# The sum over scan directions: former directions added by TensorE in the collecting bank, the result copied out by ScalarE one unit later

## The chip, the cores and the metric

The kernel runs on one core of a Trainium2 chip. The metric is the device time of one launch in microseconds; the time before is the median of three runs. A core has TensorE (PE in the profile, its weight loads PEld), VectorE (DVE), ScalarE (ACT), GpSimd (POOL) and SyncE (SP), which here issues nearly all DMAs. Each engine works through its own instructions in order and waits on semaphores for the others.

## The reference, cut to what matters

Four layers are applied in turn to a batch of four images of 96 channels and 64 by 64 pixels: an attention, a selective scan block with gates and convolutions (layer 1), a sharpening convolution, and a second selective scan block (layer 3). What the change touches is the same in layers 1 and 3: a recurrence is run over the 4096 pixels in four orders, and the four results are added at each pixel.

```python
def step(h, inp):
    d, uu, bb, cc = inp
    h = h * jnp.exp(d[..., None] * A) + (d * uu)[..., None] * bb[:, :, None, :]
    y = jnp.einsum('bkdn,bkn->bkd', h, cc)
    return (h, y)
...
return jnp.moveaxis(ys, 0, -1) + u * D[None, :, :, None]
...
y = oy[:, 0] + inv[:, 0] + why + invwhy
```

Here `oy[:, 0]` is the order by rows, `why` by columns, and `inv` and `invwhy` the same two from the last pixel to the first. There are 192 channels (two halves of 96) and 16 states for each channel. Layer 1 has `+ Ds` in place of `u * D`, a constant for each channel.

## The kernel before, in words

`streams` holds one long schedule, written out by hand. There are eight scans, one for each image and layer (`SCANS`, line 37). A scan has 32 groups: four directions, four chunks of 1024 pixels, two halves of the channels (`groups`, line 1929). A group has 12 units, each for 8 channels with their 16 states on 128 partitions; so there are 3072 units. Layer 1 takes its directions in the order rows forward, rows back, columns forward, columns back; layer 3 takes columns forward, columns back, rows forward, rows back (`KINDS`, line 1927).

A unit `i` does this (`unit`, line 2160). A DMA brings the step sizes, spread over 128 partitions (`rep`, 512 KB, `fetch`, four units ahead). ScalarE takes their exponential (`decays`, two units ahead). TensorE spreads the input over 128 partitions into a PSUM tile (`drive`, two bf16 matmuls into `bx`, two units ahead). VectorE multiplies `bx` by B in place (`times_b`, line 2086, one unit ahead) and runs the recurrence (`scan`, line 2093). GpSimd multiplies by C (`times_c`, line 2105). ScalarE keeps the last column for the next chunk (`carry_on`, line 2101). After every fourth unit TensorE adds up the 16 states of four units into the PSUM tile `acc` (`collect`, lines 2107 to 2123). `acc` has one buffer. Of a group's three collects the first starts the sums and the last ends them; since they come five units late, those of group `g` fall into the units 5 and 9 of the group and 1 of the next.

When a group's sums are complete, `output` (line 2125) makes the image `yo` [128 x 1024] of them, and SyncE stores it at the start of the next unit (`store`, line 2141):

- In a back direction (128 of the 256 groups) the sum of the direction before has been read back from HBM into `yo` (line 2114, issued with the group's first collect), and VectorE adds `acc`, read in reverse (line 2132).
- In layer 3's rows forward (32 groups) `yo` has been loaded with the input `u` (line 2117), and VectorE forms `u * D + acc` (line 2138).
- In columns forward (64 groups) ScalarE copies `acc` (line 2134), and in layer 1's rows forward (32 groups) ScalarE copies it and adds the constant D (line 2136).

There is one `yo`. The output is the last thing that a unit issues on its engine but for the work below.

Beside the units runs other work: the layers before and after the scans of other images (`BESIDE`, line 38), as Python generators that are advanced in slots. A generator yields nothing after matmuls, a number after the steps that follow them, and a tuple inside a convolution. What may be begun in a unit is set by a budget: each unit adds `PACE[s]` us of TensorE's time to what is owed (line 2268, capped at 0.6 us carried over), and `mm` (line 1017) books the cost of each matmul in `spent`, 0.853 us for an f32 matmul of 512 columns. `prepare` makes the inputs of the group after next in the same slots. What is left of a scan's side work 19 units before the scan's end is issued at once (line 2266, `at == per - NG - LEAD - 1`, unit 365 of 384). `weave` (line 1307) interleaves several generators, as in `skip` (line 1694), of which four run at a time: a convolution and Silu, a matmul and Relu, a matmul and Tanh into its own PSUM tile (line 1710, followed by `yield 0.5`), and a VectorE step that reads that tile (line 1712). Side work and `prepare` share two PSUM tiles, `one`.

Of the kernel before, what the change touches and what calls it, by code (L numbers as in the profile page):

```python
# [9 lines left out]
F32 = mybir.dt.float32  # L10
BF16 = mybir.dt.bfloat16
AF = mybir.ActivationFunctionType
ALU = mybir.AluOpType
# [16 lines left out]
PCH = 512  # L30
# [870 lines left out]
def streams(ctx: ExitStack, tc: tile.TileContext, x, wts, cst, out, wat, cat, flag):  # L901
# [3 lines left out]
    nc = tc.nc  # L905
    keep = ctx.enter_context(tc.tile_pool(name="keep", bufs=1))
# [20 lines left out]
    def cv(name):  # L927
        n, m, shape = cat[name]
        return _view(ct, (n if n < n0 else n - n1 + n0, m, shape))
# [65 lines left out]
    ident, group = cv("ident"), cv("group")  # L995
# [14 lines left out]
    spent = [0.0]  # L1010

    def full(v):

        (step, _), *rest = v.ap
        return bass.AP(v.tensor, v.offset, [(step, 128), *rest])

    def mm(o, lhsT, rhs, first=True, last=True):

        lhsT, rhs = lhsT[:], rhs[:]
        if lhsT.shape[0] == 96 and lhsT.tensor.name in padded and rhs.tensor.name in padded:  # L1020
            lhsT, rhs = full(lhsT), full(rhs)
        n = 1
        for d in rhs.shape[1:]:
            n *= d
        m = o.shape[0]
        passes = 1 if rhs.dtype == BF16 else 1.07 if m == 32 else 2 if m == R + 2 * N else 4
        spent[0] += n * passes / 2400
        nc.tensor.matmul(o, lhsT=lhsT, rhs=rhs, start=first, stop=last)  # L1028
# [56 lines left out]
    decay, dsum = {}, {}  # L1085
    top_rate = derived(4, 2)
    with Stack(1) as T:
        t0 = T.tile([128, cst.shape[1] - n2], F32, name="t0")
        nc.scalar.dma_start(out=t0, in_=cst[:, n2:])
        n, m, shape = wat["l1_alog"]  # L1090
# [4 lines left out]
        n, m, shape = cat["spread"]  # L1095
        nc.vector.tensor_copy(spread.rearrange("p a b -> p (a b)"), t0[:, n - n2 : n - n2 + m])
        for tag in ("l1_", "l3_"):
            decay[tag] = keep.tile([128, 4, E // 8], F32, name=tag + "decay")
            n, m, shape = cat[tag + "alogn"]
# [207 lines left out]
    def weave(made, depth):  # L1307

        left, active = list(made), []
        while left or active:  # L1310
            if left and len(active) < depth:
                active.append(left.pop(0))
            for g in list(active):
                while True:
                    try:
                        v = next(g)
                    except StopIteration:
                        active.remove(g)
                        break
                    yield v  # L1320
                    if v is not None and not isinstance(v, tuple):
                        break

    def attention(b, xn, w, samp, dist):
# [442 lines left out]
    def finish(PX, b, V, blocks):  # L1767

        with Stack(2) as pool:
# [140 lines left out]
            for j in range(8):  # L1910
# [14 lines left out]
    NG = 96 // 8  # L1925
# [3 lines left out]
    groups = [(s, b, tag, k, axis, back, c, h) for s, (tag, b) in enumerate(SCANS)  # L1929
              for k, axis, back in KINDS[tag] for c in range(NCH) for h in range(2)]  # L1930
    carry = keep.tile([128, 2, NG], F32, name="carry")
    yo = keep.tile([128, CH], F32, name="yo")
    nc.gpsimd.memset(yo, 0.0)
    sums = keep.tile([96, len(SCANS), 4, 2, 2 * NCH], F32, name="sums")
# [3 lines left out]
    low, ready, live = {}, {}, {}  # L1938

    def time(t, back, j0, n):  # L1940

        if not back:
            return t[:, j0 : j0 + n]
        a = t.shape[1] - 1 - j0
        return t[:, a : (a - n if a >= n else None) : -1]

    def natural(c, back):
        return bass.ts(NCH - 1 - c if back else c, CH)
# [106 lines left out]
    def place(i):  # L2055


        g, m = divmod(i, NG)
        return g, m % 4 * 3 + m // 4

    def fetch(i):

        g, m = place(i)
        rep = sp.tile([128, CH], F32, name="rep", bufs=12)
        nc.sync.dma_start(out=rep, in_=ready[g][1][8 * m : 8 * m + 8, :].unsqueeze(0).to_broadcast([N, 8, CH]))
        live[i] = [rep]

    def decays(i):
        g, m = place(i)
        k, h = groups[g][3], groups[g][7]  # L2070
        tag = groups[g][2]
        a = live[i][0]
        nc.scalar.activation(a, a, AF.Exp, scale=decay[tag][:, k, NG * h + m : NG * h + m + 1])  # L2073

    def drive(i):

        g, m = place(i)
        parts = ready[g][0]
        bx = ps.tile([128, CH], F32, tag="bx", name="bx")
        for e in range(2):  # L2080
            mm(bx[:, bass.ts(e, PCH)], spread[:, m % 4, :], parts[:, m // 4, bass.ts(e, PCH)])
        live[i].append(bx)

    def times_b(i):
        bx = live[i][1]
        nc.vector.tensor_mul(bx, bx, ready[i // NG][2][:, 0, :])  # L2086

    def scan(i):
        g, m = divmod(i, NG)
        c, h = groups[g][6:]  # L2090
        a, bx = live[i]
        hs = sp.tile([128, CH], F32, name="hs", bufs=3)
        nc.vector.tensor_tensor_scan(out=hs, data0=a, data1=bx, initial=carry[:, h, m : m + 1] if c else 0.0,  # L2093
                                     op0=ALU.mult, op1=ALU.add)
        live[i] = a, hs

    def carry_on(i):
        g, m = divmod(i, NG)
        c, h = groups[g][6:]
        if c < NCH - 1:  # L2100
            nc.scalar.copy(carry[:, h, m : m + 1], live[i][1][:, CH - 1 : CH])  # L2101

    def times_c(i):
        a, hs = live[i]
        nc.gpsimd.tensor_tensor(a, hs, ready[i // NG][2][:, 1, :], ALU.mult)  # L2105

    def collect(i):

        g, m = divmod(i, NG)
        s, b, tag, k, axis, back, c, h = groups[g]  # L2110
        if m == 0:
            live["acc"] = ps.tile([128, CH], F32, tag="acc", name="acc", bufs=1)
            if back:
                nc.sync.dma_start(out=yo, in_=(y_row if axis == "r" else y_col)[h][b][:, natural(c, back)])
            elif axis == "r" and tag == "l3_":
                for q in range(4):
                    nc.sync.dma_start(out=yo[32 * q : 32 * q + 24],
                                      in_=u_row[h][b][24 * q : 24 * q + 24, natural(c, back)])
        hs = [live.pop(i + q)[0] for q in range(4)]
        w = addn[:, 24 - 8 * (m // 4) : 56 - 8 * (m // 4)]  # L2120
        for e in range(2):
            for q in range(4):
                mm(live["acc"][bass.ts(q, 32), bass.ts(e, PCH)], w, hs[q][:, bass.ts(e, PCH)], m == 0, m == NG - 4)

    def output(i):

        g, m = divmod(i, NG)
        s, b, tag, k, axis, back, c, h = groups[g]
        dst = (y_row if axis == "r" else y_col)[h][b][:, natural(c, back)]
        ya = time(live["acc"], back, 0, CH)  # L2130
        if back:
            nc.vector.tensor_add(yo, yo, ya)
        elif axis == "c":
            nc.scalar.copy(yo, ya)
        elif tag == "l1_":
            nc.scalar.activation(yo, ya, AF.Identity, bias=dsum[tag][:, h : h + 1])
        else:
            nc.vector.scalar_tensor_tensor(out=yo, in0=yo, scalar=dsum[tag][:, h : h + 1], in1=ya,
                                           op0=ALU.mult, op1=ALU.add)
        ready.pop(g)  # L2140
        return lambda: nc.sync.dma_start(out=dst, in_=yo)

# [1 line left out]
    DRIVE, SUM, SLOT = 0.43, 1.71, 0.5  # L2144
    total = len(groups) * NG
    per = total // len(SCANS)
    store, waiting, stored, owed = [], [], [0], 0.0

    def later(n, f):

# [2 lines left out]
    def catch_up(n):  # L2153
        for w in waiting:
            w[0] -= n
        for w in [w for w in waiting if w[0] <= 0]:
            waiting.remove(w)
            w[1]()

    def unit(i, prep, work, budget):  # L2160


        if i + AHEAD < total:
            fetch(i + AHEAD)
        while store:
            store.pop()()
            stored[0] += 1
        catch_up(1)
        j = i - BEHIND - 3
        due = j >= 0 and j % 4 == 0  # L2170
        left = budget - DRIVE - (SUM if due else 0.0)
        mine = 1 <= prep.slots <= 3
        left -= prep.begin(1.0) if mine else work.begin(left)
        if i + 2 < total:
            decays(i + 2)
        scan(i)
        if i:
            carry_on(i - 1)
        times_c(i)
        if i + 1 < total:  # L2180
            times_b(i + 1)
        if mine:
            prep.end()
        work.end()
        left -= work.begin(left)
        if due:
            collect(j)
        if i + 2 < total:
            drive(i + 2)
        work.end()  # L2190
        left -= work.begin(left)
        if due and j % NG == NG - 4:
            store.append(output(j))
        work.end()
        if not mine:
            prep.begin(1.0)
            prep.end()
        return left
# [41 lines left out]
    with tc.manual_schedule():  # L2240
# [15 lines left out]
        for i in range(total):  # L2256
            s, at = divmod(i, per)
            g, m = divmod(i, NG)
            if at == 0:
                work, owed = Slots(beside(s)), 0.0  # L2260
# [7 lines left out]
            owed = min(owed, 0.6) + PACE[s]  # L2268
            owed = unit(i, prep, work, owed)
# [16 lines left out]
    m = small.tile([128, 1], F32, name="worst_1")  # L2286
# [3 lines left out]
    w = small.tile([1, 2], F32, name="worst_2")  # L2290
# [35 lines left out]
```

## Time and profile before

| what | value |
|---|---|
| median of 3 runs | 13741.8 us (13741.55 to 13748.16) |
| the profiled execution | 13771.14 us, of which the span 13769.2 us |
| granted TensorE clock over the span | 0.901 |
| the eight scans | 647.7 to 13644.7 us of the span |
| GpSimd busy | 10280.4 us (75%) |
| DMA | 2682.51 MB, 195 GB/s |

The span runs from the first to the last instruction. Busy times of one engine are unions of its instructions; TensorE's ends are modelled, and its records overlap one another. In the lists of groups the columns are: line, engine, operation, output and inputs with their shapes, the count, then busy us and mean ns of one, then the idle time of the engine ahead of them and who ended it. All matmuls have line 1028, that of their helper; `acc<-rep,ct` are the collects, `bx<-parts,spread` the drives, `one<-...` and `held<-...` side work. An f32 matmul of the program stands as two records (768 collects of 8 matmuls are 12288 records), a bf16 one as one (3072 drives of 2 are 6144).

### The profile page before, as it was taken

How to read it: one execution, taken by the hardware profiler on the slowest of the kernel's cores; microseconds unless marked ns; L12 is line 12 of the kernel's file. 1: busy time of each engine (PE TensorE's matmuls, PEld its weight loads, DVE VectorE, ACT ScalarE, POOL GpSimd, SP SyncE). 2: the span in 40 equal slices, each digit the busy share in tenths (PEclk: the TensorE clock that was granted, in tenths of full speed). 3: DMA queues.
4: the chain of work that ended last, by engine and by line, in shares of the span. 5: the costliest groups of instructions: out<-in, count | busy, mean ns of one | idle time of the engine just before them, and what ended most of it. 6: DMA issues, size and time to landing. Idle time of an engine off the chain costs nothing. (4 is left out here: it accounts for less than half of the span.)

```text
span 13769.2 us, 128385 instructions
## 1 busy us (share of the span) xinstructions
PE 11150.4 (81%) x40802; PEld 3349.2 (24%) x40802; DVE 11633.7 (84%) x7509; ACT 8718.5 (63%) x12338; POOL 10280.4 (75%) x4730
## 2 busy tenths in 40 slices
PE   9888886988779896888868887898969887777756
PEld 3322221322223221222212221232313222111111
DVE  1488998998889988889988898898889988887886
ACT  3366576667756676665766566667756676665654
POOL 1178887888878877788877888787878878666674
PEclk9899998999889897999989998998979998888867
DMA  0277788787878888778877788797888878777674
GB/s 11 68 172 197 200 224 215 201 218 203 224 195 223 210 210 212 188 194 214 232 190 198 195 216 227 192 228 198 213 214 204 224 201 229 185 196 188 172 195 115
DMA packets 840849, 2682.51 MB, mean 195 GB/s; under 512 B 111264, under 2 KB 113792, under 8 KB 840160
## 3 DMA queue, kind: packets, MB, share of 16 engines
q1 hardware_dynamic: 839504, 2672.34, 76.2%
q8 instruction: 324, 5.31, 0.2%
q14 instruction: 365, 2.99, 0.1%
q10 hardware_dynamic: 656, 1.87, 0.0%
HBM read 2179.90 MB, written 493.88 MB: 194 GB/s over the span
## 5 line engine op out<-in xcount | busy, mean ns | idle before, releaser
L2105 POOL TENSOR_TENSOR rep<-hs,bc 128x1024 f32<-128x1024 f32 x3072 | 7221.1, 2357 | 2404.3 <-DVE hs L2093 2012.5
L1028 PE MATMUL one<-arena 128*96 128x512 f32 (+5 forms) x11072 | 5294.0, 604 | 583.9 <-ACT arena L1394 134.2
L2093 DVE TENSOR_TENSOR_SCAN hs<-rep,carry,bx 128x1024 f32<-128x1024 f32 x2304 | 5400.8, 2344 | 302.1 <-ACT rep L2073 36.2
L2086 DVE TENSOR_TENSOR bx<-bx,bc 128x1024 f32<-128x1024 f32 x3072 | 3717.8, 1210 | 683.6 <-PE bx L1028 677.9
L2073 ACT ACTIVATE rep<-rep,l_decay 128x1024 f32<-128x1024 f32 x3072 | 3496.2, 1143 | 764.1 <-DMA rep<-dd 743.3
L1028 PE MATMUL bx<-parts,spread 128*128 128x512 bf16 x6144 | 2030.3, 415 | 1338.7 <-DVE hs L2093 1225.9
L1028 PEld LDWEIGHTS one<-arena 128*96 128x96 f32 (+4 forms) x11072 | 1793.8, 172 | 3053.6 <-issue 1783.9
L2093 DVE TENSOR_TENSOR_SCAN hs<-rep,bx 128x1024 f32<-128x1024 f32 x768 | 1754.5, 2285 | 138.6 <-ACT carry L2101 57.8
L1028 PE MATMUL acc<-rep,ct 128*32 128x512 f32 x12288 | 1721.9, 674 | 7.0 <-POOL rep L2105 7.0
L1028 PEld LDWEIGHTS <-spread 128*128 128x128 bf16 x6144 | 446.9, 100 | 3663.4 <-DVE hs L2093 2374.3
L1028 PE MATMUL one<-pr,ct 64*96 64x512 f32 x1024 | 628.5, 698 | 76.1 <-ACT pr L1980 27.0
L1394 ACT ACTIVATE arena<-one 128x512 f32<-128x512 f32 x576 | 342.2, 594 | 495.3 <-PE one L1028 493.7
L1028 PEld LDWEIGHTS acc<-rep,ct 128*32 128x32 f32 x12288 | 359.4, 118 | 1169.3 <-issue 944.6
L2073 ACT ACT_TABLE_LOAD x492 | 631.2, 1283 | 8.8
L2101 ACT COPY carry<-hs 128x1 f32<-128x1 f32 x2304 | 408.7, 177 | 219.6 <-DVE hs L2093 216.9
L1028 PE MATMUL bx<-arena 128*96 128x512 f32 (+5 forms) x1120 | 489.2, 575 | 21.3 <-ACT arena L1808 3.2
L1028 PE MATMUL one<-arena,ct 128*96 128x512 f32 x508 | 293.9, 686 | 255.3 <-ACT arena L1546 194.5
L1028 PE MATMUL held<-arena,cols 128*32 128x256 f32 x3072 | 481.2, 395 | 12.3 <-ACT arena L1394 11.5
L1028 PE MATMUL held<-arena 128*32 128x256 f32 x3072 | 481.7, 395 | 0.0
L982 POOL MEMSET arena<- 32x1024 f32 (+5 forms) x81 | 54.0, 690 | 393.6 <-ACT arena L1394 321.5
L2015 ACT ACT_TABLE_LOAD x256 | 328.4, 1283 | 4.4
L1028 PE MATMUL one<-us,wt 128*38 128x512 f32 x1024 | 282.3, 674 | 49.1 <-DMA us<-urow 23.7
(3322 smaller groups left out, 9879.5 us busy)
## 6 DMA issues: line engine op xcount, KB each, us to landing
rep<-dd SPq DMA_DIRECT2D x3072, 512.0 KB
parts<-du SPq DMA_DIRECT2D x1024, 144.0 KB
bc<-rows SPq DMA_DIRECT2D x256, 512.0 KB
dd<-delta SPq DMA_DIRECT2D x256, 384.0 KB
du<-cut SPq DMA_DIRECT2D x256, 384.0 KB
yrow<-yo SPq DMA_DIRECT2D x128, 512.0 KB
ycol<-yo SPq DMA_DIRECT2D x128, 512.0 KB
us<-urow SPq DMA_DIRECT2D x128, 384.0 KB
```

Source lines behind the costliest of these rows:

```text
L982: nc.gpsimd.memset(arena[96:, k : min(k + CH, a + n)], 0.0)
L1028: nc.tensor.matmul(o, lhsT=lhsT, rhs=rhs, start=first, stop=last)
L1394: nc.scalar.activation(last.rearrange("p a b -> p (a b)"), p, AF.Exp, scale=HD**-0.5)
L2015: nc.scalar.activation(w, w, AF.Ln)
L2073: nc.scalar.activation(a, a, AF.Exp, scale=decay[tag][:, k, NG * h + m : NG * h + m + 1])
L2086: nc.vector.tensor_mul(bx, bx, ready[i // NG][2][:, 0, :])
L2093: nc.vector.tensor_tensor_scan(out=hs, data0=a, data1=bx, initial=carry[:, h, m : m + 1] if c else 0.0, op0=ALU.mult, op1=ALU.add)
L2101: nc.scalar.copy(carry[:, h, m : m + 1], live[i][1][:, CH - 1 : CH])
L2105: nc.gpsimd.tensor_tensor(a, hs, ready[i // NG][2][:, 1, :], ALU.mult)
```

## The change

A new function `former(i)` lets TensorE add the image in `yo` to `acc` between the second and the third collect: two f32 matmuls of 128 x 128 by 512 columns, with the identity as weights in back directions (and `yo` read in reverse), and a diagonal of D in layer 3's rows forward. It is issued at the head of the unit in which the third collect is two units away (unit 11 of the group), and what it books is taken from that unit's budget. `output` is then a copy by ScalarE in all groups (with the constant D in layer 1's rows forward), and no step of VectorE is left in it. It is issued one unit later than before, behind that unit's `decays` and ahead of its `scan`; the store moves one unit later with it. In `weave`, a step that yields 0.5 no longer passes the turn to the next generator. Two VectorE instructions ahead of the scans make the diagonals.

```diff
@@ weave
-                    if v is not None and not isinstance(v, tuple):
+                    if v is not None and not isinstance(v, tuple) and v != 0.5:
                         break
@@
+    skipped = keep.tile([128, 2, 128], F32, name="skipped")
+    for m in range(2):
+        nc.vector.tensor_scalar(skipped[:, m, :], ident, dsum["l3_"][:, m : m + 1], None, ALU.mult)
@@
+    def former(i):
+
+        g = i // NG
+        s, b, tag, k, axis, back, c, h = groups[g]
+        if back or (axis == "r" and tag == "l3_"):
+            w = ident if back else skipped[:, h, :]
+            for e in range(2):
+                mm(live["acc"][:, bass.ts(e, PCH)], w, time(yo, back, e * PCH, PCH), False, False)
+
@@ output
-        if back:
-            nc.vector.tensor_add(yo, yo, ya)
-        elif axis == "c":
-            nc.scalar.copy(yo, ya)
-        elif tag == "l1_":
+        if axis == "r" and tag == "l1_" and not back:
             nc.scalar.activation(yo, ya, AF.Identity, bias=dsum[tag][:, h : h + 1])
         else:
-            nc.vector.scalar_tensor_tensor(out=yo, in0=yo, scalar=dsum[tag][:, h : h + 1], in1=ya,
-                                           op0=ALU.mult, op1=ALU.add)
+            nc.scalar.copy(yo, ya)
@@ unit
+        if j > 0 and j % NG == 6:
+            t = spent[0]
+            former(j)
+            left -= spent[0] - t
         mine = 1 <= prep.slots <= 3
         left -= prep.begin(1.0) if mine else work.begin(left)
         if i + 2 < total:
             decays(i + 2)
+        while made:
+            store.append(output(made.pop()))
         scan(i)
@@
         if due and j % NG == NG - 4:
-            store.append(output(j))
+            made.append(j)
```

More of the change, by code (lines that the diff above doesn't have):

```diff
@@ L2146, in streams @@
     per = total // len(SCANS)
-    store, waiting, stored, owed = [], [], [0], 0.0
+    made, store, waiting, stored, owed = [], [], [], [0], 0.0
     def later(n, f):
```

## The prediction

> **What bounds the kernel now.** I read four views. First the page's busy times:
>
> ```profile
> PE 11150.4 (81%) x40802; PEld 3349.2 (24%) x40802; DVE 11633.7 (84%) x7509; ACT 8718.5 (63%) x12338; POOL 10280.4 (75%) x4730
> ```
>
> VectorE and TensorE are nearly level, so an average decides nothing. Second, the groups of instructions with their shapes kept apart:
>
> ```profile
> L2093 DVE TENSOR_TENSOR_SCAN hs<-rep,carry,bx 128x1024 f32<-128x1024 f32 x2304 | 5400.8, 2344 | 302.1 <-ACT rep L2073 36.2 <-ACT carry L2101 15.1 <-POOL rep L2105 5.0
> L2086 DVE TENSOR_TENSOR bx<-bx,bc 128x1024 f32<-128x1024 f32 x3072 | 3717.8, 1210 | 683.6 <-PE bx L1028 677.9 <-DMA rep<-dd 1.2
> ...
> L2132 DVE TENSOR_TENSOR yo<-yo,acc 128x1024 f32<-128x1024 f32 x128 | 155.9, 1218 | 83.9 <-PE acc L1028 81.8
> ...
> L2134 ACT COPY yo<-acc 128x1024 f32<-128x1024 f32 x64 | 64.3, 1004 | 53.0 <-PE acc L1028 52.5
> L2138 DVE SCALAR_TENSOR_TENSOR yo<-yo,l_dsum,acc 128x1024 f32<-128x1024 f32 x32 | 40.8, 1276 | 27.2 <-PE acc L1028 26.9
> L2136 ACT ACTIVATE yo<-acc,l_dsum 128x1024 f32<-128x1024 f32 x32 | 35.3, 1104 | 12.6 <-PE acc L1028 12.4
> ```
>
> A unit costs VectorE 2.34 + 1.21 = 3.55 us. From the starts of the 3072 scan instructions the median distance of two units is 3.60 us, the mean of the first seven scans 4.11: the typical unit is VectorE's, and 0.5 us a unit is lost in long ones, where VectorE mostly waits for TensorE's `bx` (678 us). Third, a group's end on VectorE:
>
> ```profile
> 1149.46 2.29 DVE L2093 TENSOR_TENSOR_SCAN hs<-rep,bx 128x1024 f32<-128x1024 f32 x1
> 1152.55 1.23 DVE L2086 TENSOR_TENSOR bx<-bx,bc 128x1024 f32<-128x1024 f32 x1 [0.81 <-PE bx L1028]
> 1155.80 1.22 DVE L2132 TENSOR_TENSOR yo<-yo,acc 128x1024 f32<-128x1024 f32 x1 [2.02 <-PE acc L1028]
> 1156.94 2.28 DVE L2093 TENSOR_TENSOR_SCAN hs<-rep,bx 128x1024 f32<-128x1024 f32 x1
> ```
>
> The next scan stands behind the add, the add behind the third collect. In scans 0 to 6 the distance from the group's second scan instruction to its third is 5.43 us where VectorE makes the output and 4.11 where ScalarE does. But the rest of the group gives time back, so 1.3 us is not the price.
>
> Fourth, busy times in stretches. Layer 3's rows forward are made by VectorE where layer 1, at the same place of its scan beside the same work, has ScalarE copy columns forward. So the kernel itself holds a trial of one engine against the other. Seven groups each, of scans 1, 2, 5, 6, 4, 3:
>
> ```profile
> 3097.36:3440.21 342.85, 300.50 (x958) 92.02 (x956) 299.32 (x183) 255.36 (x344) 278.69 (x127) 0.92 0.79 202
> 4667.69:5014.53 346.84, 301.49 (x958) 91.23 (x956) 307.21 (x190) 251.64 (x339) 278.86 (x127) 0.91 0.83 210
> 9408.39:9751.57 343.18, 300.65 (x956) 91.83 (x954) 299.21 (x184) 255.16 (x343) 278.69 (x127) 0.91 0.79 202
> 10981.88:11328.71 346.83, 301.70 (x960) 91.34 (x958) 307.27 (x191) 251.81 (x339) 278.82 (x127) 0.92 0.82 210
> 7870.27:8193.84 323.57, 273.38 (x898) 82.93 (x898) 300.37 (x186) 191.25 (x272) 274.19 (x124) 0.93 0.84 212
> 6286.86:6617.07 330.21, 271.08 (x899) 81.44 (x898) 309.17 (x193) 184.13 (x264) 274.44 (x124) 0.93 0.85 215
> ```
>
> Columns: length, then busy us of PE, PEld, DVE, ACT, POOL. Scan 2 against 1: DVE +7.89 us, length +3.99. Scan 6 against 5: +8.06, +3.65. Scan 3 against 4: +8.80, +6.64. So 0.51, 0.45 and 0.75 of VectorE's output time comes through; per output 0.57, 0.52 and 0.95 us. Over whole scans (1579.84 against 1577.33, 1576.73 against 1574.24, 1581.22 against 1578.92, eight outputs more) only 0.3 us each. And where the side work is layer 1's second half (scans 1, 2, 5, 6), TensorE is as busy as VectorE: 300 of 343 us.
>
> **VectorE's outputs go (160 groups).** Removed: 155.9 + 40.8 = 196.7 us of work and 83.9 + 27.2 = 111.1 us of waits, 308 us in all if everything came through. Bounds: 0.3 x 160 = 48 below, 308 above. I take the trial in place, half of the work: 98 us. What is late next is `bx` from TensorE, which gives back the other half. The trial has ScalarE's copy in it, so that is paid for too.
>
> **ScalarE copies all outputs.** 160 x 1.0 = 160 us more on an engine at 63%. [...] Reversed copies by ScalarE are in no row; VectorE's reversed add at 1218 ns is nothing out of the way, so the same 1.0. Behind the copy on ScalarE stand `carry_on` and the evictions that free the `one` tiles; that is inside the trial. Moved one unit later, the copy no longer waits for the collect (53.0 + 12.6 us before): those waits lie on an engine with slack, so 0 to 20 us gain; I take 5. `acc` stays taken longer: the copy will come behind `decays`, whose end is 2.3 us after the unit's scan starts (median, 6.7 at the 95th percentile), and the next group's first collect is three units on; nothing.
>
> **TensorE's formers.** Its own rows give the price:
>
> ```profile
> 4644.96 3.60 PE L1028 MATMUL one<-arena 128*96 128x512 f32 x8
> ```
>
> Eight records in 3.60 us, the last about 0.6 long, are 0.43 apart; an f32 matmul is two records, so a former is 4 x 0.43 = 1.72 us, and 160 of them 275 us. [...] Reversed reading costs nothing: half of `one<-us,wt` is reversed, and its least and its median record are both 592 ns. Where do 275 us go? They are taken from the unit's budget, so no unit gets more matmuls; side work ends later. By the planner of before, side work ends at unit 355, 344, 344, 354, 354, 344, 344 of scans 0 to 6; behind that it books 1.1 us a unit. Side work gets about 1.8 us a unit at a pace of 2.95 and 2.3 at 3.45. Formers ahead of unit 365: 14 in layer 1 (24 us), 22 in layer 3 (38 us). So side work ends 13 units later in scans 0 and 4, 21 in scan 3, 10 in 1 and 5, 16 in 2 and 6. A unit with side work takes 4.05, one without 3.87: 84 of these 99 units lie ahead of unit 365, 84 x 0.2 = 17 us. Scans 0, 4 and 3 pass unit 365 by 3, 2 and 10 units, and 27 us of matmuls would be issued in one lump; budget that is now forfeited at the cap (18 us in each of these scans) takes up part. I take 14, bounds 0 and 27. Scan 7 has slack: from unit 281 on the work is idle in 46 units for want of stored sums.
>
> The former waits for `yo`'s load. Before, TensorE came to that place 17 us or more after the load's issue (median 28); the store and so the load come up to 4 us later. ScalarE saw `rep`, of the same size, land 4.4 to 15.2 us after issue where it waited for it (median 9.0). So a wait of 2 us in one in twenty at most, with `drive` and so VectorE behind it: 3 us, bounds 0 and 16. SyncE's queue: its store waits for the output already (2685 us over 237 stores), with the fetches behind it. The store passes one fetch more and is released some 3.3 us later, a unit being 3.6 to 4.1: nothing either way.
>
> **The turn at 0.5.** In `skip`, Tanh holds one of two `one` tiles until VectorE's step, which comes up to 17 us later since other generators have their turn. TensorE waits for that step 20 us in all; VectorE waits for `bx` 13 to 19 us in each such stretch (units 226 to 262 of scans 1, 2, 5, 6). Taking the step at once gives up to 66 us back, or makes VectorE wait for Tanh, up to 1.5 us x 32 = 48. I take 8 gained, near the row of 20.
>
> **Start and tail.** Two small steps ahead of the scans, the last output 1.0 for 1.22: nothing.
>
> **Sum.** -98 - 5 + 17 + 14 + 3 - 8 = -77 us. Against the profiled execution, 13771.1 - 77 = 13694; the median of the runs is 29.3 us (0.2%) below that execution, so 13741.8 - 77 = 13665.
>
> **Rivals.** *All of it comes through*: VectorE bounds each unit (median 3.60 against 3.55 of work), the 308 us vanish: 13741.8 - 308 + 21 = 13455. Against it: the trial, where half came back. *It is given back*: 0.3 us an output as over whole scans, 48 us, less the same 21: 13715, at the edge of what could be told. *TensorE takes VectorE's place*: the booked budget is already all that TensorE can give where it is 300 of 343 us busy; then each former stands ahead of a `drive`, and costs 1.72 less the 0.61 saved. In the 80 groups of scans 1, 2, 5, 6 that is +89, the other 80 give -49, and 21 more: 13803. It decides once TensorE's real time in the units round a former is over the 3.60 us of VectorE; for it speak the 678 us of waits for `bx`, against it that groups with more booked matmuls (40 and over: 46.6 us) are no slower than those with 33 to 36 (48.9).
>
> **Chances.** Forecast 0.50, all through 0.13, given back 0.19, TensorE 0.18. A measurement can tell about 0.2%, 27 us. Faster: 0.50 + 0.13 and a sliver of the third, 0.66; same 0.16; slower 0.18. The range reaches half into the first and the last rival, 13540 to 13785; the forecast's own, with its bounds, is 13610 to 13715.
>
> **What would show it.** Right: no `yo` row on VectorE and 197 us less of it; 640 records `acc<-yo` at 0.43 us pitch; the trial's stretches of scans 2 and 6 within 1 us of 1 and 5; side work longer in each scan; waits for `bx` higher than 678. Wrong: PE waits on `yo<-yrow` or `yo<-ycol` beyond 16 us, `bx` waits up by more than 200 us, a stall at unit 365 of scan 3 beyond 20 us, or `acc<-rep` waiting for ScalarE's copy.

## The result, and the profile after

The median went from 13743.5 us (8 runs, 13733.43 to 13753.89) to 13699.7 us (8 runs, 13694.06 to 13715.87): a ratio of 0.9968, 95% interval 0.9959 to 0.9978, or 44 us less. The forecast was 77 us less (13665). The profiled execution of after took 13707.96 us, 8 over its median; that of before lay 28 over its own, so a comparison of the two profiles shows some 20 us too much gain.

The page's busy times after the change:

```profile
PE 11203.6 (82%) x40767; PEld 3476.9 (25%) x41442; DVE 11460.3 (84%) x7351; ACT 8833.5 (64%) x12480; POOL 10278.9 (75%) x4730
```

VectorE does 173 us less (the outputs' 197 us went; other rows differ by the rest) and 158 fewer instructions: 160 outputs less, two diagonals more. The span is 63 us shorter in these profiles, so nearly two thirds of VectorE's saving is not in the time. The groups with shapes apart (columns as before):

```profile
L2096 DVE TENSOR_TENSOR_SCAN hs<-rep,carry,bx 128x1024 f32<-128x1024 f32 x2304 | 5401.9, 2345 | 312.5 <-ACT carry L2104 31.8 <-POOL rep L2108 18.6 <-DVE bx L2089 7.3
L2089 DVE TENSOR_TENSOR bx<-bx,bc 128x1024 f32<-128x1024 f32 x3072 | 3719.9, 1211 | 816.8 <-PE bx L1028 547.8 <-PE acc L1028 121.8 <-PE one L1028 90.3
...
L1028 PE MATMUL acc<-yo,ct 128*128 128x512 f32 x512 | 254.3, 621 | 1.7 <-issue 0.9
L2146 ACT COPY yo<-acc 128x1024 f32<-128x1024 f32 x224 | 222.6, 994 | 83.8 <-PE acc L1028 83.6
...
L1028 PE MATMUL acc<-yo,skipped 128*128 128x512 f32 x128 | 61.8, 606 | 0.2
L2144 ACT ACTIVATE yo<-acc,l_dsum 128x1024 f32<-128x1024 f32 x32 | 35.1, 1097 | 8.5 <-PE acc L1028 8.5
```

The `yo` rows of VectorE are gone, and the formers stand there as 512 + 128 = 640 records. They waited 1.9 us in all, so no load of `yo` came late. A copy by ScalarE costs 994 ns, reversed ones included. VectorE's idle time ahead of its multiplication went from 683.6 to 816.8 us: this is the largest part of what was lost. Two smaller parts are the recurrence, with idle time ahead of it up from 440.7 to 469.4 us, and the step of `skip` that now waits for its Tanh at once, where before it had no idle time ahead of it:

```profile
L1712 DVE SCALAR_TENSOR_TENSOR arena<-one,arena 96x512 f32<-96x512 f32 x32 | 21.9, 685 | 58.3 <-ACT one L1710 58.3
```

675 records of `bx<-parts,spread` are missing in this trace (5469 of 6144), so a wait for `bx` is partly put down to the TensorE record before it, `acc` or `one`; the three releasers together are 547.8 + 121.8 + 90.3 = 760 us, against 678.

The end of the group that the prediction shows, on VectorE, in the timeline of after:

```profile
1146.44 1.23 DVE L2089 TENSOR_TENSOR bx<-bx,bc 128x1024 f32<-128x1024 f32 x1 [0.81 <-PE bx L1028]
1147.81 2.29 DVE L2096 TENSOR_TENSOR_SCAN hs<-rep,bx 128x1024 f32<-128x1024 f32 x1
1150.01 1.21 DVE L2089 TENSOR_TENSOR bx<-bx,bc 128x1024 f32<-128x1024 f32 x1
1151.35 2.29 DVE L2096 TENSOR_TENSOR_SCAN hs<-rep,bx 128x1024 f32<-128x1024 f32 x1
```

No output stands between a multiplication and the next scan instruction any more, and the second scan instruction starts 3.5 us after the first. Over the whole kernel the distance from the second unit of a group to its third shrank by 253 us. But the distances that follow in the group grew: by 99.7, 19.1, 51.3, 40.5, 65.3 and 46.8 us for those that start at its third, fourth, fifth, sixth, eighth and ninth unit; the other five shrank by 127 us together. Last, the trial's stretches of seven groups, in the order of before (scans 1, 2, 5, 6, 4, 3):

```profile
3088.32:3433.39 345.07, 298.40 (x953) 93.14 (x969) 300.27 (x186) 250.24 (x340) 277.06 (x122) 0.94 0.79 203
4664.39:5024.64 360.25, 309.97 (x961) 96.88 (x977) 301.70 (x187) 247.43 (x336) 276.57 (x122) 0.91 0.78 201
9403.27:9748.68 345.41, 297.06 (x952) 93.06 (x968) 299.56 (x187) 249.30 (x339) 277.01 (x122) 0.93 0.78 202
10971.40:11326.71 355.31, 305.81 (x961) 95.81 (x977) 301.27 (x186) 248.15 (x337) 277.41 (x122) 0.92 0.80 204
7862.85:8180.17 317.32, 273.18 (x888) 83.27 (x903) 299.49 (x183) 182.05 (x259) 273.89 (x120) 0.95 0.86 215
6280.19:6590.78 310.59, 275.89 (x915) 85.63 (x931) 297.83 (x180) 176.52 (x240) 273.58 (x120) 0.99 0.90 229
```

VectorE's busy time (third pair) is now level within 2 us from scan to scan, as it should be. The lengths (first number behind the stretch) are not: scan 2 is 15 us longer than scan 1 and 13 longer than it was, while scan 3 is 20 shorter than it was. Part of that is other work in the same units: the first Tanh of `skip` lies at unit 235 in all four scans of before, and at 241, 243, 241 and 243 after. So stretches by units compare unlike work, and from here on half scans are compared.

### The profile page after: what moved, and what is told of

Same layout as the page of the kernel before. It is cut to its first block, busy times and chain, and to the rows that moved or that the text cites. A ratio compares the mean times of both kernels' runs of the same rounds, so it can differ in the third digit from the quotient of the medians.

```text
span 13706.2 us, 129052 instructions
## 1 busy us (share of the span) xinstructions
PE 11203.6 (82%) x40767; PEld 3476.9 (25%) x41442; DVE 11460.3 (84%) x7351; ACT 8833.5 (64%) x12480; POOL 10278.9 (75%) x4730
## 4 chain that ended last, share of the span: by engine, by line
PE 30%; DVE 15%; ACT 14%; DMA 10%; POOL 6%; issue 6%; SPq 1%; DVEq 0%; POOLq 0%; ACTq 0%; another core or an unknown queue 0%
PE one L1028 21%; DVE hs L2096 9%; DMA rep<-dd 5%; PE acc L1028 5%; DVE bx L2089 4%; PE bx L1028 4%; ACT rep L2076 3%; POOL rep L2108 3%; ACT L2076 1%; ACT L2018 1%; DMA arena<-ycol 1%; DMA du<-cut 1%; ACT arena L1394 1%; PE held L1028 1%; DMA parts<-du 1%
## 5 line engine op out<-in xcount | busy, mean ns | idle before, releaser
L1028 PE MATMUL one<-arena 128*96 128x512 f32 (+4 forms) x11072 | 5276.8, 602 | 640.1 <-ACT arena L1394 140.4
L2089 DVE TENSOR_TENSOR bx<-bx,bc 128x1024 f32<-128x1024 f32 x3072 | 3719.9, 1211 | 816.8 <-PE bx L1028 547.8
L1028 PE MATMUL bx<-parts,spread 128*128 128x512 bf16 x5469 | 1828.1, 408 | 1054.9 <-DVE hs L2096 954.9
L1028 PEld LDWEIGHTS one<-arena 128*96 128x96 f32 (+3 forms) x11072 | 1787.4, 171 | 3062.7 <-issue 1763.9
```

## Experiments

"Gain" is a kernel's median against that of the kernel before, measured beside it (13743.5 to 13759.6). The four kernels without the formers' matmuls (outputs moved alone; moved, and the turn; one unit later; booked, not issued) leave the addition of the former directions out: they show what a part costs and could not take the change's place. The intervals of the ratios are about 18 us to either side (13 and 12 where more runs were made), so a difference between two experiments is known to some 25 us.

| kernel | median us | ratio, interval | gain us |
|---|---|---|---|
| the change | 13699.7 | 0.9968 (0.9959 to 0.9978) | 44 |
| turn alone | 13707.7 | 0.9969 (0.9957 to 0.9981) | 42 |
| outputs moved alone | 13678.1 | 0.9942 (0.9928 to 0.9955) | 75 |
| moved, and the turn | 13629.9 | 0.9912 (0.9896 to 0.9927) | 123 |
| the same, one unit later | 13645.7 | 0.9926 (0.9913 to 0.9940) | 104 |
| the same later, formers booked, not issued | 13673.8 | 0.9943 (0.9930 to 0.9957) | 76 |
| formers issued, not booked | 13745.7 | 0.9999 (0.9990 to 1.0008) | 4 |
| the change, output in the old unit | 13666.8 | 0.9935 (0.9922 to 0.9949) | 93 |
| the change, output ahead of `decays` | 13688.4 | 0.9950 (0.9937 to 0.9964) | 67 |
| the change, former in two halves | 13740.4 | 0.9987 (0.9978 to 0.9996) | 19 |
| the change, the budget given back | 13699.2 | 0.9963 (0.9950 to 0.9977) | 54 |
| change in the last scan only, turn everywhere | 13661.9 | 0.9932 (0.9919 to 0.9946) | 91 |
| the same, output in the old unit | 13680.1 | 0.9942 (0.9929 to 0.9956) | 80 |

**The turn alone.** The kernel before with one condition more.

```diff
-                    if v is not None and not isinstance(v, tuple):
+                    if v is not None and not isinstance(v, tuple) and v != 0.5:
```

> The kernel before with one line of the change: a step that yields 0.5 keeps the turn. The prediction has 8 us gained (bounds 66 gained, 48 lost): 13736 beside 13743 of the kernel before, no change that can be told. A rival holds that this line is what pays for the rest: then 13700 or less.

It gained 42 us, in the profile nearly all of it in scans 1, 2, 5 and 6 (14.0, 13.8, 7.0 and 10.0 us). The timelines of a Tanh (L1710) and the VectorE step that frees its PSUM tile (L1712), before:

```profile
3298.36 0.66 ACT L1710 ACTIVATE one<-one,der 96x512 f32<-96x512 f32 x1 [0.34 <-PE one L1028]
...
3312.52 0.68 DVE L1712 SCALAR_TENSOR_TENSOR arena<-one,arena 96x512 f32<-96x512 f32 x1
```

and with the turn:

```profile
3288.81 0.64 ACT L1710 ACTIVATE one<-one,der 96x512 f32<-96x512 f32 x1
...
3289.49 0.69 DVE L1712 SCALAR_TENSOR_TENSOR arena<-one,arena 96x512 f32<-96x512 f32 x1 [2.80 <-ACT one L1710]
```

From the end of the Tanh to the step it was 13.5 us and is now 0.04; over all 32 steps the mean was 7.8 us and is 0.3. The waits of VectorE in the 36 units of `skip` in scan 1, before:

```profile
DVE bx L2086 <- PE bx L1028: 19.4, 12, 5.2
```

and with the turn:

```profile
DVE arena L1712 <- ACT one L1710: 12.3, 6, 3.5
DVE bx L2086 <- PE bx L1028: 3.5, 4, 2.6
```

In the four stretches the waits for `bx` fell from 66.2 to 16.9 us and 38.3 us of waits for Tanh came, so 11 us are gained there (12 by the lengths of the stretches). Another 33 us are gained in the 78 units behind, where no `skip` runs any more and `bx` was waited for 90.3 us before and 64.1 now. Why the later units gain was not traced to an instruction.

**Outputs moved alone.** ScalarE copies all outputs in their old unit; no turn, no former.

```diff
-        if back:
-            nc.vector.tensor_add(yo, yo, ya)
-        elif axis == "c":
-            nc.scalar.copy(yo, ya)
-        elif tag == "l1_":
+        if axis == "r" and tag == "l1_" and not back:
...
+            nc.scalar.copy(yo, ya)
```

> The kernel before with nothing but VectorE's outputs replaced by ScalarE's copies in the same unit: no turn, no formers, no booking; it leaves the addition of the former directions out. This is the trial of scans 3 and 4, 2 and 1, 6 and 5 done for all 160 outputs. If 0.61 us an output come through as the prediction took it, 13651. If what was measured between the turn alone and the kernel without formers holds (62 us), 13687. If all of VectorE's work and waits were worth their time, 13441.

It gained 75 us, 0.47 for each of 160 outputs, of the 308 us of work and waits that left VectorE. The distance from a group's second unit to its third fell by 254 us, as in the change. So the gain does come through at its place, and in this profile 165 us of it are given back at the other units of the groups without any former.

**Moved, and the turn.** The change without former and booking, the output in the old unit.

```diff
-            former(j)
-            left -= spent[0] - t
+            pass
...
-            made.append(j)
+            store.append(output(j))
```

> The kernel with the turn and all outputs copied by ScalarE, without formers and booking, but each output in the unit of its last collect as before, not one unit later; it leaves the addition of the former directions out. One unit later it took 13646 (0.9926 of before). If the move to a later unit helps (ScalarE no longer waits for the collect), this is slower, 13660 to 13680. If the later copy is what kept the saving below the 98 us of the trial in place, this is faster, 13600 to 13625.

The gain of 123 us is the sum of the two alone (75 + 42 = 117), within what two experiments can tell: nothing shows that they get in each other's way.

**The change with the output in the old unit.** The second of these two edits alone, so the whole sum is computed.

> The changed kernel with each output copied in the unit of its last collect, as before, and not one unit later. Without formers the later unit cost 16 to 19 us (13646 against 13630, each beside its own kernel before: 104 and 123 us gained). If that loss is its own, this is 13680 to 13688, 0.995 to 0.996 of before. If the later unit makes up for the formers (the collect comes later on TensorE, so ScalarE would wait for it), this is no faster than the changed kernel, 13700 to 13720.

A gain of 93 us. Against the kernel above, formers and their booking cost 30 us. Against the change, the later unit costs 49 us by the gains and 33 by the two medians.

**One unit later, without formers.** The change with `pass` for the former and its booking.

> The changed kernel without the matmuls of former and without their booking; it leaves the addition of the former directions out. Theory A (what the formers do to TensorE and to the budget took back some 60 us; the move off VectorE alone is worth 0.74 us an output, about 110 us): 13620 to 13650. Theory B (the move itself is worth no more than the 44 us that were measured, since TensorE's collect is late next in any case): 13690 to 13705. In the profile A expects the units from 340 on of scans 0, 3 and 4 to be as short as before, B the same as in the changed kernel.

104 us, 19 less than in the old unit, which is within what two experiments can tell.

**Booked, not issued.** As above, but the budget of those units is lowered by what a former would book.

```diff
+            if back or (axis == "r" and tag == "l3_"):
+                left -= 2 * PCH * 4 / 2400
```

> The same without the matmuls, but with 1.71 us taken from the budget where they would be, so the side work ends as late as in the changed kernel (unit 365 with 6, 18 and 6 us of matmuls in one lump in scans 0, 3, 4); it leaves the addition of the former directions out. If the later end of the side work is the cost (A1), this is as slow as the changed kernel, 13690 to 13705. If TensorE's time in the units of the formers is (A2), this is as fast as the one without formers and booking, 13620 to 13650.

The booking alone costs 28 us (13645.7 to 13673.8), between the two sizes that were expected. The stretches of units 340 to 383 of scan 3 show the lump at unit 365; before, then after:

```profile
6819.52:6984.94 165.42, 105.55 (x355) 24.62 (x353) 152.63 (x89) 101.54 (x126) 138.75 (x61) 0.76 0.92 237
```

```profile
6788.89:6978.47 189.58, 140.87 (x447) 41.86 (x454) 149.71 (x86) 117.77 (x144) 142.81 (x63) 0.85 0.83 214
```

92 matmul records more (the count behind the first busy time; 13 of them are formers'), 24 us longer. But the side work's share of them is missing from earlier units of the same scan, which got shorter, and scan 3 as a whole is 8 us shorter than before. In the two profiles with and without booking the cost lies elsewhere: +37 us in the second halves (units 204 to 383) of scans 1, 2, 5 and 6, where TensorE is nearly as busy as VectorE (600 against 631 of 722 us in scan 2), and less than nothing in scans 3, 4 and 7. Scan 2, units 204 to 383, without booking and with it:

```profile
4625.65:5347.62 721.97, 600.28 (x1936) 179.76 (x1934) 630.67 (x375) 529.03 (x696) 592.24 (x263) 0.88 0.84 220
```

```profile
4651.56:5387.18 735.62, 603.57 (x1965) 184.05 (x1963) 630.74 (x377) 531.52 (x697) 591.28 (x263) 0.91 0.84 217
```

29 matmul records more and 14 us longer, with VectorE's work the same.

**Issued, not booked.** The change without the subtraction.

```diff
-            t = spent[0]
             former(j)
-            left -= spent[0] - t
```

> The changed kernel with the formers issued but nothing taken from the budget for them; side work ends at the units of the kernel before, and a unit with a former has up to 1.71 us more of matmuls. A1 (the later end of the side work costs, some 55 us): 13640 to 13660. A2 (TensorE's time in those units costs): 13700 to 13760, with longer waits for bx in unit 11 and unit 0 of a group.

Nothing is left of the gain: 100 us worse than without formers, 0.63 us for each of 160, and 40 worse than booked. So what a former takes of TensorE's time does count, and the booking, which costs 28 us, avoids more than that.

**The former in two halves.** One matmul at the head of unit 11 and one at that of the next group's first unit, each booked.

```diff
-        if j > 0 and j % NG == 6:
+        if j > 0 and j % NG in (6, 7):
...
-            former(j)
+            former(j, (j % NG - 6,))
```

> The changed kernel with the former's two matmuls issued in two units, 10 wait, one each: the first half at the head of unit 11, the second at the head of unit 0 of the next group, 0.85 us booked in each. The matmuls cost 26 us beside the same booking without them. If it is a lump of 1.7 us in one unit ahead of that unit's drive that delays VectorE, halves cost less: 13675 to 13690. If it is TensorE's time as such, 13695 to 13710.

13740.4 us, 41 worse than the former in one piece (25 by the gains). This speaks against a lump of two matmuls in one place that holds up `drive`: halves were expected to cost less then. Why they cost more stays open.

**The output ahead of `decays`.** Still one unit later, but issued before that unit's exponential.

```diff
+        while made:
+            store.append(output(made.pop()))
         if i + 2 < total:
             decays(i + 2)
-        while made:
-            store.append(output(made.pop()))
```

> The change with one statement moved: the output's copy, still one unit later than before, is issued ahead of that unit's `decays`, not behind it; the store and all else stay. The whole sum over the directions is computed. With the output in the old unit the kernel took 13666.8 us (92.9 under the kernel before), one unit later 13699.7 (44 under). Theory A: the later unit costs its 33 to 49 us because the copy stands behind an exponential that itself waits for the step sizes from HBM, so that acc and what stands behind the copy on ScalarE come later; then this kernel lies within 10 us of the old place: 80 to 95 under the kernel before, some 13670. Theory B: it costs them since in the next unit the copy stands behind the side work's ScalarE steps and its store is issued a unit later, whatever the order against `decays`; then this kernel stays with the change, 35 to 55 under. The waits of ScalarE for the loads of rep (962 us in the change, 933 in the old place) would not move by A or B alone.

67 us, between the two theories, with an interval that overlaps those of both kernels that it stands between. It settles nothing.

**The budget given back.** `PACE` raised by about what the formers book on average, 0.08 us in the scans of layer 1 and 0.12 in those of layer 3 but the last (16 and 24 formers of 1.71 us over 384 units are 0.07 and 0.11).

```diff
-PACE = (2.95,3.45,3.45,2.95,2.95,3.45,3.45,3.2)
+PACE = (3.03,3.53,3.57,3.07,3.03,3.53,3.57,3.2)
```

> The changed kernel with the pace of scans 0 to 6 raised by 0.08 (layer 1) and 0.12 us a unit (layer 3), which gives back what the formers take from the budget, so that side work ends near the units of the kernel before and no lump is left at unit 365. If the later end of the side work costs the 28 us that lie between booking and no booking, this is 13670 to 13685. If TensorE has no more time to give (as with the formers not booked, 13746), it is no faster than the changed kernel, 13700 to 13725.

13699.2 against 13699.7 by the medians, 54 against 44 us by the gains: not told apart from the change. The 13670 to 13685 that were expected if the later end of the side work were the cost did not come. That the fuller units take what the shorter end gives would fit, but is not shown.

**The change in the last scan only.** Formers and later outputs by ScalarE in scan 7, outputs as before in the others, the turn everywhere. Then the same with the output in the old unit in scan 7 too.

```diff
-        if back or (axis == "r" and tag == "l3_"):
+        if s == len(SCANS) - 1 and (back or axis == "r"):
             w = ident if back else skipped[:, h, :]
...
+        if back and s < len(SCANS) - 1:
+            nc.vector.tensor_add(yo, yo, ya)
```

> The turn everywhere, but formers and ScalarE's later outputs only in the last scan; scans 0 to 6 have VectorE's outputs as before. In the profiles the last scan is 50 us shorter in the changed kernel, and scans 0 to 6 lie 39 us above those of the kernel with the turn alone. If the change pays where VectorE's own side work is four times as long and the budget has waits to give (scan 7), this is the fastest of the full kernels: 13708 - 48, 13650 to 13670. If scan 7's gain hangs on how scans 0 to 6 end, it is 13690 to 13710.

> The kernel with the turn everywhere and formers in the last scan alone, its outputs copied by ScalarE in the same unit as before. If the later unit costs 0.1 us an output, the 32 outputs of the last scan give 3 us and this is not told apart from 13662 (0.9932). If the last scan gained by the later store and the later start of the work that waits for it, this is slower, 13670 to 13690.

91 and 80 us. Of the 91, 42 are the turn's; the other 49 go with the 24 outputs of one scan that were moved. By the profiles scan 7 took 1926.2 us before, 1924.6 with the turn alone, 1883.8 here (41 of the 49), and 1876.4 in the change. Scans 0 to 6 together took 11070.7 us before, 11023.9 with the turn alone, and 11063.1 in the change: in these seven scans formers and later outputs cost some 39 us more than they win, and by the medians, too, taking them out of those scans gains 38. This kernel and the change with the output in the old unit, both of which compute the whole sum, are the fastest of those that do: 38 and 33 us under the change, and not told apart from each other.

The later unit without the turn was not measured.

## Why the prediction was right, and where its sum was wrong

The sign held and the size in the rough: 44 us of gain against 77, with 13700 inside the forecast's own range of 13610 to 13715. That the total came so near is in good part luck. The turn, which has nothing to do with the sum over directions and was foretold at 8 us, gains 42 alone, so the whole change is not told apart from it: moving the outputs won 75 us, and the later unit, the booking and the matmuls took 79 back, where the prediction had 29 for them. By a path through the experiments, each step against the one before it, the measured sum, whose steps are each known to some 25 us, is -75 (moved) - 48 (turn) + 19 (later unit) + 28 (booking) + 32 (the formers' matmuls) = -44. Point by point:

- **VectorE's outputs go: -98 foretold, -75 measured.** The reasoning held: the trial inside the kernel gave the right kind of answer, far from the 308 us of work and waits. The step that went wrong is that half of the work came through; it was 0.47 us an output and not 0.61, still between the 0.3 of whole scans and the trial. "What is late next is `bx` from TensorE" is what the profiles show: with the outputs moved alone VectorE's waits for it, put down to `bx`, `acc` and `one`, are 566.6 + 98.2 + 87.6 = 752 us, against 678 before.
- **ScalarE's copy.** The rows of before held: 1.00 us foretold, 0.99 measured, reversed or not (984 to 1014 ns), where VectorE's add took 1.22; with the 160 copies on ScalarE 75 us of gain are left.
- **Moved one unit later: -5 foretold, +19 measured without formers, +33 to +49 with them.** This is the term with the wrong sign. The prediction argued it free since the next group's first collect is three units on and ScalarE has slack. By the profiles, 30 us are lost in the first halves of scans 1, 2, 5 and 6 and 25 in the second; the distances that start at the group's fifth unit grow by 87 us in all and those that start at its fourth shrink by 53. No wait of `acc<-rep` is put down to the copy (the engine named is GpSimd, 156.7 us in 190 waits). VectorE's waits for `bx`, by the same three releasers, are 760 us against 671 with the output in the old unit, those of the recurrence for `carry` 86 against 123; why `bx` comes later is open. That it stands behind `decays` is not shown: putting it ahead recovered 11 to 23 us, with an interval that overlaps those of both.
- **The formers' matmuls: 0 beside the booking foretold, +3 for the load; measured +32** by the gains, 26 by the two medians. The load cost nothing, as the 1.9 us of waits say. The step that failed is "they are taken from the unit's budget", so free beyond it: the budget settles how much else is begun in the unit, not that the matmuls find idle time there.
- **Side work ends later: +17 and +14 foretold, +28 measured.** The size agrees, the place does not. The planner of the change ends the side work of scans 0 to 6 at units 365, 354, 360, 365, 365, 354 and 360 against the 368, 354, 360, 375, 367, 354 and 360 foretold, with lumps of 6, 18 and 6 us in scans 0, 3 and 4. The lump of scan 3 shows (24 us), but the same scan had got it back before; the cost is in the second halves of scans 1, 2, 5 and 6. A sum that agrees can be made of the wrong parts.
- **The turn: -8 foretold, -42 measured (-48 on top of the moved outputs).** The mechanism was right (in the stretches the waits for `bx` fell by 49 us and 38 us of waits for Tanh came) and the bounds of -66 to +48 held it; the size was off fivefold. The prediction set the 20 us that TensorE waited for the step beside the waits for Tanh, and so saw only what happens in the stretch itself, where 11 us were measured. The larger part, 33 us, came in units behind it. Without this term the steps above add up to 4 us of loss, no change that could be told; this sum was not run as a kernel.

**The rivals.** *All of it comes through* is out: 0.47 us an output. *It is given back* (13715) had its rate for an output too low, 0.3, and its total nearly right, since other costs took what the better rate gave. *TensorE takes VectorE's place* did not come about with the booking, but unbooked the formers bring the kernel back to 13746, 100 us worse than without them; that they do so by standing ahead of a `drive` was not shown. Of the signs that the prediction named, two went against it: the stretches of scans 2 and 6 are 15 and 10 us longer than those of 1 and 5 and not level, and the stall at unit 365 was over 20 us and yet was not a loss. The waits for `bx` rose by 82 us, more than 0 and under the 200 that would have spoken against.

## What to carry to other kernels

When a step leaves the busiest engine and a second one is nearly as busy, look for a place in the same kernel where both ways already stand side by side, take that rate, and then price every move that comes with it (order, unit, booking) as if it could cost as much as the gain: here the three additions took back 79 of 123 us. A budget that a planner keeps is not idle time: the booking alone cost 28 us and the matmuls within it 32 more, and by the profiles the cost of the booking lay where TensorE is nearly as busy as VectorE (600 against 631 of 722 us in scan 2). And a PSUM tile held over a turn of an interleaved schedule (7.8 us for a step of 0.7) can be worth more than half of an arithmetic step removed 160 times: 42 us here against 75.

## What was not expected of the hardware

The granted TensorE clock of the profiled executions was 0.901 before and 0.903 with the turn or the moved outputs alone, 0.905 to 0.908 in the other kernels without formers in scans 0 to 6 and without booking, but 0.912 with the booking alone, 0.912 with the formers unbooked, and 0.917 in the change, with the output in either unit. So the time of after was taken at a granted clock 1.8% higher; what that is worth in time, and what raises the clock, none of the runs tells.
